# Later places for three steps of the block matching: two transposes and a group of maxima, put one or two turns further on

## The chip, the cores and the metric

The kernel runs on one core of one Trainium2 chip. The metric is the device time of that core in microseconds (us), the median of several executions. One more execution is recorded by the hardware profiler, and all durations below come from that one.

## The reference, cut to what matters

The input `x` holds 8 images of 32 channels with 128 x 128 pixels. The first layer compares every pixel's 3x3 patch with those at the 25 places of a 5x5 window, takes the 8 nearest, gathers their pixels (256 channels), and runs a small convolutional net on them. The second layer is one 5x5 convolution.

```python
def _patch_match_stack(x):
    for dy in range(-2, 3):
        for dx in range(-2, 3):
            sh = x[:, :, yy][:, :, :, xx]                     # shifted, clipped
            d = ((x - sh) ** 2).sum(1, keepdims=True)         # distance
            costs.append(_conv(d, ones, pad=1))               # 3x3 sum
    _, idx = jax.lax.top_k(-jnp.transpose(cost, (0, 2, 3, 1)), 8)
    g = ...                                                   # x at the 8 places
    return ...                                                # [B, 256, H, W]

xb = _patch_match_stack(_gn(x))
dct = _conv(xb, dct_w, groups=32)
h = relu(_conv(_conv(xb, w1), w2, groups=256, pad=1))         # pointwise, depthwise
h = relu(_conv(_conv(h, w3), w4, groups=256, pad=1))
wiener = sigmoid(_conv(_conv(h, w5), w6, groups=256, pad=1))
x = x + _conv(_conv(wiener * dct, inv_dct_w, groups=32), agg_w)
x = x + conv5x5(_gn(x))
```

## The kernel before, in words

**Steps and turns.** The images are worked through one after the other, each in 17 steps of 8 rows. All steps of all images form one list, and the main loop (L1015) goes over it. One step has four **turns** (L1026, `for i in (3, 2, 1, 0)`): turns 3, 2 and 1 do the third, second and first pointwise and depthwise layer, each on a step that lies that much further back, and turn 0 does the last stage. An image thus has 68 turns. In each turn TensorE (PE) has about this order: the pointwise product of the upper 128 channels (`pv`, L641); what the former turn 0 left over (`pa`, L798); then the loose tasks of the queue "P"; in turn 0 the product with the DCT weights (`pc`, L777); the pointwise product of the lower channels (`p`, L665); one unit of the gather (`pg`, L603); and the depthwise layer of the lower channels of the turn before (`pw`, L718). VectorE (DVE) does the depthwise layer of the upper channels: eight multiply-adds on a tile of 128 x 1024 (`acc`, L695), one group in each of the turns 3, 2 and 1. In turn 0 it multiplies `acc` by `pc` (L785). ScalarE (ACT) copies PSUM tiles out, prepares the selection tiles of the gather (L588, L589) and applies the depthwise layer's function (`acc`, L699).

**The order is written out by hand.** PE, DVE and ACT execute their instructions in the order in which the Python program emits them (`manual_schedule(engines=ORDERED)`, L999). Waits between engines follow from the tiles that are written and read. GpSimd (POOL) and SyncE (SP) only issue DMAs and fill borders.

**Loose tasks.** The block matching of the next image is spread over the turns of the current one. It is written as generators. `yield "P", 0` parks a task in the queue for PE, `yield "D", 1.85` in that for DVE with a cost of 1.85 us, `yield "A"` in that for the end of a turn. A third value tells how many turns must go by at least before the task may go on. `run("P")` takes all due tasks of its queue. `tick` (L984) counts a turn, adds an allowance to `owed`, and takes tasks of "D" in their order of arrival until it is spent. In one turn, `run("P")` stands ahead of `tick`. A task that was parked in a tick is taken up by `run("P")` at the start of the next turn.

**The steps around the change.** An image's distances are handled in four chunks (`i` = 0 to 3) of 8 rows in each quarter of the image.

- `costs` loads a chunk's squared differences into `dsum`, waits three turns, and sums 3x3 neighbours on DVE (L477 to L489) by way of a tile `v`. It then transposes the result on PE in two halves of four rows (`pt`, L494, `h` = 0 and 4). ACT copies each half out (`ct`, L498). DVE searches it in four tasks of eight instructions each (`mx` and `idx`, L505 and L506).
- `places` then turns the chunk's indices into addresses on DVE (L520 to L529, tile `oc`), transposes them on PE (`pi`, L538), copies them on ACT (`li`, L540) and stores them with two DMAs from POOL's queue (L541). The gather of the next image reads them back much later.

`v` (L474) and `oc` (L517) are allotted from one pool under one tag with a single buffer:

```python
v = work.tile([P, R, W + 2], F32, name=f"v_{b}_{i}", tag="v", bufs=1)      # L474
oc = work.tile([P, R, W + 2], F32, name=f"oc_{b}_{i}", tag="v", bufs=1)    # L517
```

Only one chunk at a time can be in `dsum`: `held` is set at L459 and cleared when the second half is transposed (L496).

PSUM tiles of PE's products (`pv`, `p`, `pg`, `pa`, `pc`, `pt`, `pi`) come from one pool of five buffers, `ps_x`.

Of the kernel before, what the change touches and what calls it, by code (L numbers as in the profile page):

```python
# [15 lines left out]
P = 128  # L16
# [26 lines left out]
def bm3d_conv_preact(  # L43
# [172 lines left out]
    def push(task):  # L216
        want = next(task, None)
        if want:
            which, cost, *wait = want
            queues[which].append((cost, task, now[0] + (wait[0] if wait else 0)))  # L220
# [181 lines left out]
    def squares(b, i, pd, xn, aa, sq, idx):  # L402
# [48 lines left out]
        if q is not None:  # L451
            push(costs(b, q, sq, idx))

    def costs(b, i, sq, idx):

        yield "A", 0, 2
        while held:
            yield "A", 0, 1
        held.add(b)  # L459

        nc.gpsimd.dma_start(
            dsum[52:100, :, 1 : 1 + W],
            sq[:, :, 8 * i + 2 : 8 * i + 4 + R, 2 : 2 + W].rearrange("o g r x -> (o g) r x"),
        )
        for o in range(13, NO):
            dy, dx = o // 5 - 2, o % 5 - 2
            p = 4 * (NO - 1 - o)
            nc.gpsimd.dma_start(
                dsum[p : p + 4, :, 1 : 1 + W],
                sq[o - 13, :, 8 * i + 2 - dy : 8 * i + 4 + R - dy, 2 - dx : 2 - dx + W],  # L470
            )
        yield "D", 4.6, 3

        v = work.tile([P, R, W + 2], F32, name=f"v_{b}_{i}", tag="v", bufs=1)  # L474
        cost = dsum[:, 0:R, 1 : 1 + W]
        r0 = 1 if i == 0 else 0
        nc.vector.tensor_add(v[:, r0:], dsum[:, r0:R], dsum[:, r0 + 1 : 1 + R])  # L477
        if i == 0:
            nc.vector.scalar_tensor_tensor(
                v[:, 0], dsum[:, 0], inner[:, 0:1], dsum[:, 1], op0=ALU.mult, op1=ALU.add  # L480
            )
        r1 = R - 1 if i == 3 else R
        nc.vector.tensor_add(v[:, :r1], v[:, :r1], dsum[:, 2 : 2 + r1])
        if i == 3:
            nc.vector.scalar_tensor_tensor(
                v[:, r1], dsum[:, R + 1], inner[:, 1:2], v[:, r1], op0=ALU.mult, op1=ALU.add
            )
        nc.vector.tensor_add(cost, v[:, :, 0:W], v[:, :, 1 : 1 + W])
        nc.vector.tensor_add(cost, cost, v[:, :, 2 : 2 + W])  # L489
        for h in range(0, R, 4):  # L490
            yield "P", 0
            pt = ps_x.tile([P, 4, P], F32, name=f"pt_{b}_{i}_{h}", tag="x")
            for q in range(4):
                nc.tensor.transpose(pt[:, q], cost[:, h + q], ident)  # L494
            if h:
                held.clear()  # L496
            ct = work.tile([P, 4, P], F32, name=f"ct_{b}_{i}_{h}", tag="ct")
            nc.scalar.copy(ct[:, :, 0 : 4 * NO], pt[:, :, 0 : 4 * NO])  # L498
            mx = work.tile([P, 16, K], F32, name=f"mx_{b}_{i}_{h}", tag="mx")
            for q in range(4):  # L500
                yield "D", 1.85
                y = 8 * i + h + q
                for rg in range(4):
                    c25 = ct[:, q, rg : rg + 4 * NO - 3 : 4]
                    nc.vector.max(mx[:, 4 * q + rg], c25)  # L505
                    nc.vector.max_index(  # L506
                        idx[:, rg, y // 4, :, y % 4], mx[:, 4 * q + rg], c25
                    )
        push(places(b, idx, i))

    def places(b, idx, i):


        if i == 0:
            idxd[b] = dram.tile([4, 8, K * 4, W], BF16, name=f"idxd_{b}", tag="idxd")
        yield "D", 2.6
        oc = work.tile([P, R, W + 2], F32, name=f"oc_{b}_{i}", tag="v", bufs=1)  # L517
        oc = oc.rearrange("p r w -> p (r w)")
        o, ct = oc[:, 0:256], oc[:, 256:512]
        nc.vector.tensor_copy(  # L520
            o.rearrange("p (g z) -> p g z", g=4),
            idx[:, :, 2 * i : 2 * i + 2].rearrange("p g s k y -> p g (s k y)"),
        )
        nc.vector.tensor_scalar(ct, o, 5.0, None, op0=ALU.is_ge)
        for lim in (10.0, 15.0, 20.0):
            nc.vector.scalar_tensor_tensor(ct, o, lim, ct, op0=ALU.is_ge, op1=ALU.add)
        nc.vector.scalar_tensor_tensor(o, ct, float(QW - 5), o, op0=ALU.mult, op1=ALU.add)
        o3 = o.rearrange("p (s y) -> p s y", y=4)
        nc.vector.tensor_tensor(  # L529
            o3,  # L530
            o3,
            cst[:, C_BASE : C_BASE + 4].unsqueeze(1).to_broadcast([P, 64, 4]),
            ALU.add,
        )
        yield "P", 0
        for h in range(2):
            pt = ps_x.tile([P, 512], F32, name=f"pi_{b}_{i}_{h}", tag="x")
            nc.tensor.transpose(pt[:, :P], o[:, h * P : (h + 1) * P], ident)  # L538
            li = work.tile([P, P], BF16, name=f"li_{b}_{i}_{h}", tag="li")
            nc.scalar.copy(li, pt[:, :P])  # L540
            nc.gpsimd.dma_start(  # L541
                idxd[b][2 * h : 2 * h + 2, 2 * i : 2 * i + 2].rearrange("g s k x -> g (s k) x"),
                li,
            )
        ready.add((b, i))
        if i == 3:
            ready.add(b)
# [451 lines left out]
    with tc.manual_schedule(engines=ORDERED):  # L999
# [15 lines left out]
        for s in range(len(steps) + 2):  # L1015
            if s < len(steps):
                b, n = steps[s]
# [120 lines left out]
```

## Time and profile before

| quantity | value |
|---|---|
| median of 3 runs | 6862.14 us (6855.92 to 6876.67) |
| the profiled execution's own time | 6856.73 us |
| its span, first to last instruction | 6855.0 us |
| granted TensorE clock, mean | 0.974 |
| PE busy | 6362.1 us, 93% of the span |
| DVE busy | 5857.0 us, 85% |
| ACT busy | 5067.7 us, 74% |
| POOL busy | 3250.0 us, 47% |

A share of busy time is a mean over the whole span. What a moved step is worth is read from the place where it stands. Two views serve for that. The waits list pairs of an idle engine and the work that ended its idle time: total us, number of times, longest us. The timeline lists each engine's instructions in order of time: start, length, engine, line, operation, tiles, count, and in brackets the idle time ahead of it and what ended that.

### The profile page before, as it was taken

The page shows a single profiled execution, that of the slowest core. Times are in us where ns is not written, and L with a number is a line of the kernel's source. Part 1 is how long each engine was busy: PE and PEld are TensorE (multiplying, and loading weights), DVE is VectorE, ACT ScalarE, POOL GpSimd, SP SyncE. Part 2 cuts the span into 40 slices and gives each one's busy share as a digit, 9 for nine tenths or more (in the row PEclk, how much of TensorE's full clock was granted, in tenths as well). Part 3 has the DMA queues.
Part 4 walks back from the last instruction along what each step waited for, and adds up shares of the span by engine and source line. Part 5 has one row for each costly group of instructions (what it writes and reads, how often), then busy time and mean ns, then how long its engine had stood idle before and what let it go on. Part 6 is the DMA issues. An engine that isn't in the chain of part 4 may idle for free.

```text
span 6855.0 us, 232443 instructions
## 1 busy us (share of the span) xinstructions
PE 6362.1 (93%) x101090; PEld 2969.2 (43%) x101090; DVE 5857.0 (85%) x8822; ACT 5067.7 (74%) x6698; POOL 3250.0 (47%) x5351
## 2 busy tenths in 40 slices
PE   4698899999999999999999999999999999999997
PEld 1344444444444444444444444444444444444443
DVE  6799988989889898988989888898988889877776
ACT  4687768777687777877778777887768777786772
POOL 6345436544464444644446444464445544344334
PEclk9899999999999999999999999999999999999998
DMA  3566656666566675665656656566665666566553
GB/s 80 134 151 148 155 134 150 163 149 162 149 155 161 147 168 134 167 145 151 165 131 165 160 145 167 134 172 152 151 153 146 161 157 149 137 164 157 148 151 79
DMA packets 809531, 1019.84 MB, mean 149 GB/s; under 512 B 255456, under 2 KB 619936, under 8 KB 808512
## 3 DMA queue, kind: packets, MB, share of 16 engines
q0 software_dynamic: 422432, 745.61, 42.4%
q1 hardware_dynamic: 381056, 256.86, 16.9%
q8 instruction: 796, 13.04, 0.8%
q10 hardware_dynamic: 5024, 2.49, 0.2%
q14 instruction: 223, 1.83, 0.1%
HBM read 553.25 MB, written 217.01 MB: 112 GB/s over the span
## 4 chain that ended last, share of the span: by engine, by line
PE 53%; DVE 20%; DMA 9%; ACT 8%; issue 6%; POOL 3%; SPq 0%; ACTq 0%; POOLq 0%; DVEq 0%
PE pw L718 19%; PE pv L641 13%; DVE acc L695 13%; PE p L665 11%; DMA t<-t 4%; PE pg L603 3%; PE pc L777 2%; PE p L891 2%; DVE idx L506 2%; ACT ib L588 2%; DVE df L413 1%; PE pd L428 1%; ACT df L421 1%; PE pa L798 1%; DVE acc L785 1%
## 5 line engine op out<-in xcount | busy, mean ns | idle before, releaser
L695 DVE SCALAR_TENSOR_TENSOR acc<-tv,dwv,acc 128x1024 f32<-128x1024 f32 (+3 forms) x3264 | 4032.8, 1237 | 255.1 <-ACT acc L692 141.7
L718 PE MATMUL pw<-t,dwd 96*32 96x508 f32 (+6 forms) x19392 | 2161.7, 593 | 137.9 <-DMA t<-t 97.4
L574 POOL DMA_DIRECT2D ib<-idxd x1024 | 571.8, 559 | 1828.0 <-ACT sel L589 1677.2
L718 PEld LDWEIGHTS pw<-t,dwd 96*32 96x32 f32 (+1 forms) x19392 | 715.7, 112 | 1265.5 <-issue 1174.2
L588 ACT ACTIVATE ib<-ib,nplace 128x1024 bf16<-128x1024 bf16 x1024 | 1170.3, 1143 | 19.1 <-DMA ib<-idxd 19.1
L589 ACT ACTIVATE sel<-ib 128x1024 f32<-128x1024 bf16 x1024 | 1084.7, 1059 | 32.5
L665 PE MATMUL p<-acc,lw 128*32 128x256 f32 x16768 | 991.3, 381 | 20.0 <-ACT tv L649 19.5
L641 PE MATMUL pv<-acc,lw 128*128 128x512 f32 (+1 forms) x2112 | 972.0, 602 | 30.2 <-DVE acc L785 22.9
L758 POOL DMA_DIRECT2D xf<-xbd x1088 | 652.8, 634 | 305.3 <-PE pc L777 80.7
L665 PEld LDWEIGHTS p<-acc,lw 128*32 128x32 f32 x16768 | 556.6, 111 | 447.8 <-ACT tv L649 59.5
L649 ACT COPY tv<-pv 128x512 f32<-128x512 f32 (+2 forms) x784 | 439.2, 578 | 403.4 <-PE pv L641 380.6
L603 PEld LDWEIGHTS pg<-sel,xt 128*32 128x32 f32 x45056 | 575.3, 111 | 260.4 <-ACT sel L589 67.1
L421 ACT ACTIVATE df<-df 128x786 f32<-128x786 f32 (+2 forms) x576 | 468.5, 860 | 291.6 <-DVE df L413 288.5
L603 PE MATMUL pg<-sel,xt 128*32 128x48 f32 x45056 | 593.5, 207 | 89.2 <-ACT sel L589 47.6
L731 ACT ACTIVATE acc<-pw 128x512 f32<-128x512 f32 (+2 forms) x808 | 442.7, 573 | 295.7 <-PE pw L718 294.9
L641 PEld LDWEIGHTS pv<-acc,lw 128*128 128x128 f32 x2112 | 380.0, 191 | 524.3 <-issue 404.4
L413 DVE TENSOR_TENSOR df<-xn 128x786 f32<-128x786 f32 (+2 forms) x576 | 527.8, 968 | 82.8 <-PE pd L428 70.9
L699 ACT ACTIVATE acc<-acc 128x1024 f32<-128x1024 f32 (+3 forms) x408 | 416.9, 1022 | 235.4 <-DVE acc L695 235.1
L672 ACT COPY t<-p 128x512 f32<-128x512 f32 x800 | 424.7, 571 | 127.8 <-PE p L665 125.8
L692 ACT ACTIVATE acc<-tv,dwv 128x1024 f32<-128x1024 f32 (+3 forms) x408 | 454.6, 1114 | 57.9 <-PE pa L798 39.1
L641 PE MATMUL pv<-xb,lw 128*128 128x512 f32 x1024 | 474.5, 606 | 0.0
L665 PE MATMUL p<-xb,lw 128*32 128x256 f32 x8192 | 467.6, 380 | 0.0
(151 smaller groups left out, 5778.6 us busy)
## 6 DMA issues: line engine op xcount, KB each, us to landing
ib<-idxd POOLq DMA_DIRECT2D x1024, 256.0 KB, 4.5
xbd<-xb POOLq DMA_DIRECT2D x128, 1024.0 KB, 6.8
xf<-xbd POOLq DMA_DIRECT2D x960, 128.0 KB, 7.0
t<-t SPq DMA_DIRECT2D x792, 128.0 KB
t<-t SPq DMA_DIRECT2D x384, 256.0 KB
tv<-tv SPq DMA_DIRECT2D x384, 130.0 KB
xt<-xtd POOLq DMA_DIRECT2D x240, 176.0 KB, 4.4
xl<-xs POOLq DMA_DIRECT2D x256, 64.0 KB, 2.5
```

Source lines behind the costliest of these rows:

```text
L413: nc.vector.tensor_sub(df[:, :, ca:cz], xn[:, r0 : r0 + SR, ca:cz], xn[:, r0 + dy : r0 + dy + SR, ca + dx : cz + dx],)
L421: nc.scalar.activation(df[:, :, ca:cz], df[:, :, ca:cz], AF.Square)
L574: nc.gpsimd.dma_start(ib.rearrange("p k y x -> p (k y x)"), idxd[b][s4 // 8, s4 % 8, 4 * k0 : 4 * k0 + 8] .rearrange("k x -> (k x)") .part ...
L588: nc.scalar.activation(ib, ib, AF.Square, bias=nplace)
L589: nc.scalar.activation(sel, ib, AF.Relu, scale=-1.0, bias=1.0)
L603: nc.tensor.matmul(pg[C * j : C * (j + 1), :, xa:xz], xt[:, t], sels[j // 2][:, j % 2, :, xa:xz], start=True, stop=True,)
L641: nc.tensor.matmul(ps[:, :hr], lhsT[:, g, P:CK], src(g)[:, h : h + hr], start=g == 0, stop=g == 1,)
L665: nc.tensor.matmul(ps[C * r : C * (r + 1), e, :nb], lhsT[:, g, s], rows[:, r : r + 4 * nb - 3 : 4], start=g == 0, stop=g == 1,)
L692: nc.scalar.activation(acc, rows, AF.Copy, scale=tap)
L695: nc.vector.scalar_tensor_tensor(acc, rows, tap, acc, op0=ALU.mult, op1=ALU.add)
L718: nc.tensor.matmul(pt[u][C * j : C * (j + 1), : nh[u], :nb, xa:xz], dwd[0:hi, i - 1, u, j, dx + 1], t[0:hi, j, : nh[u], :nb, xa + dx : xz ...
L758: nc.gpsimd.dma_start(xf[p : p + C, m, j0:j1], src[g, m, (h + m + 1) % 2, :, :, ya:yz])
```

## The change

Three values are added to three `yield` lines, all for images after the first only (`b` is not 0).

- The transpose of the first half of a chunk's distances (`pt`, `h` = 0) may go on one turn later.
- The first of the four tasks of maxima of each half may go on one turn later. The other three come after it, one by one.
- The transpose of the addresses (`pi`) may go on two turns later, and with it the copies at L540 and the two DMAs at L541.

```diff
         for h in range(0, R, 4):
-            yield "P", 0
+            yield "P", 0, 1 if b and h == 0 else 0
             pt = ps_x.tile([P, 4, P], F32, name=f"pt_{b}_{i}_{h}", tag="x")
...
             for q in range(4):
-                yield "D", 1.85
+                yield "D", 1.85, 1 if b and q == 0 else 0
                 y = 8 * i + h + q
...
-        yield "P", 0
+        yield "P", 0, 2 if b else 0
         for h in range(2):
             pt = ps_x.tile([P, 512], F32, name=f"pi_{b}_{i}_{h}", tag="x")
             nc.tensor.transpose(pt[:, :P], o[:, h * P : (h + 1) * P], ident)
```

No instruction is added or taken away, and no tile changes its size.

## The prediction, made before the changed kernel was run

> **What bounds the kernel now.** I read the page's busy shares and chain first, then the waits list, then the timeline of the places where the moved steps stand.
>
> ```profile
> PE 6362.1 (93%) x101090; PEld 2969.2 (43%) x101090; DVE 5857.0 (85%) x8822; ACT 5067.7 (74%) x6698; POOL 3250.0 (47%) x5351
> ...
> PE 53%; DVE 20%; DMA 9%; ACT 8%; issue 6%; POOL 3%; SPq 0%; ACTq 0%; POOLq 0%; DVEq 0%
> ```
>
> PE carries the time: it is idle for 6855.0 - 6362.1 = 493 us, and nothing that leaves PE's idle time as it is can help. DVE is second, and it leads in a fifth of the chain. The waits list of PE says what that idle time is.
>
> ```profile
> PE pw L718 <- DMA t<-t: 97.4, 39, 5.1
> PE pi L538 <- DVE oc L529: 56.8, 15, 20.2
> ...
> PE pv L641 <- DVE acc L785: 22.9, 15, 2.2
> ```
>
> The second line is what the change is about: PE stands still until DVE has the addresses. But most of it is image 0, which the change leaves alone. The same list from 1400 us on, images 2 to 7, has:
>
> ```profile
> PE pi L538 <- DVE oc L529: 9.0, 8, 1.3
> ```
>
> In between, in image 1, the timeline shows 1.8, 6.7 and 2.8 us. So at most 9.0 + 11.3 = 20 us of waits at `pi` can go. The wait of DVE for `ct` (L505) adds 1.3 us in each later image, and PE has no wait at `pt` there.
>
> Now the place itself: chunk 3 of one image, DVE first. The groups at L695 are one turn's depthwise layer each.
>
> ```profile
> 3303.72 0.43 DVE L529 TENSOR_TENSOR oc<-oc,cst 128x256 f32<-128x256 f32 x1
> 3304.73 1.24 DVE L477 TENSOR_TENSOR v<-dsum 128x1040 f32<-128x1040 f32 x1 [0.59 <-DMA xf<-xbd]
> ...
> 3308.68 1.23 DVE L489 TENSOR_TENSOR dsum<-dsum,v 128x1024 f32<-128x1024 f32 x1
> 3309.82 0.41 DVE L806 TENSOR_TENSOR xr<-xr,pa 128x256 f32<-128x256 f32 x1
> ...
> 3310.61 10.51 DVE L695 SCALAR_TENSOR_TENSOR acc<-tv,dwv,acc 128x1024 f32<-128x1024 f32 x8
> ...
> 3322.76 10.51 DVE L695 SCALAR_TENSOR_TENSOR acc<-tv,dwv,acc 128x1024 f32<-128x1024 f32 x8
> ...
> 3334.86 10.51 DVE L695 SCALAR_TENSOR_TENSOR acc<-tv,dwv,acc 128x1024 f32<-128x1024 f32 x8
> 3345.29 2.47 DVE L785 TENSOR_TENSOR acc<-acc,pc 128x512 f32<-128x512 f32 x4
> ```
>
> DVE has no gap from `v` to L785. PE over the same stretch:
>
> ```profile
> 3304.29 0.41 PE L538 MATMUL pi<-cst,oc 128*128 128x128 f32 x2 [0.51 <-DVE oc L529]
> ...
> 3322.86 3.70 PE L641 MATMUL pv<-xb,lw 128*128 128x512 f32 x8
> 3326.49 3.66 PE L665 MATMUL p<-xb,lw 128*32 128x256 f32 x64
> ...
> 3346.03 3.70 PE L641 MATMUL pv<-acc,lw 128*128 128x512 f32 x8 [1.61 <-DVE acc L785]
> ```
>
> At 3346 PE waits for DVE's first multiplication by `pc`. In this stretch DVE is the slower one, by 1.61 us. The other five later images show 1.6, 0.5, 1.0, 1.2 and 0.1 us there.
>
> **What the Trainium skill says.** "PSUM — Partial Sum Buffer", Engine vs sequencer instructions: "ScalarE/VectorE/GpSimdE queues are strict FIFO". A DVE instruction that waits holds up all behind it. The trace agrees: behind `v`, which started 0.59 us late, nothing overtook. "Perfetto Trace Analysis", Identifying Performance Opportunities: repeating gaps on the engine that should be full can mean too few buffers for the next tile. For PE before, only the tenths to 1.6 us above repeat at this place; what follows is a buffer of this kind that comes free later. "VectorE: DVE Perf Modes", The TRN2 errata: an fp32 add of N elements takes (N+151)/0.96 ns, which for `v` (N = 1040) is 1241 ns; L477 shows 1234. The price of the summing stays.
>
> **The change part by part.** Nothing is added or removed; all is order.
>
> *Transpose of distances, one turn on (28 chunks).* Four products, 0.60 us of PE, stand later, and `ct` (0.47 us on ACT) with them. PE had no wait there, so nothing is gained. `held` still clears with the second half. Cost 0, from -5 to +5 for other neighbours.
>
> *First maxima, one turn on.* Eight instructions of 0.19 + 0.30 us per half move to a turn in which `ct` is surely there. The 1.3 us waits stand ahead of second halves; between these two the same turn count passes as before, so they stay. Gain 0.
>
> *Transpose of addresses, two turns on.* Two products (0.41 us), two copies (0.26 us each), two DMAs of 0.82 us on POOL move past the ib loads (L574) of two turns. The first reader of the new addresses comes three or more turns after the last late store, by the turn numbers of the emission, so no gather waits. What goes is PE's wait at `pi`. What is late next is the buffer: `oc` can't be overwritten until `pi` has read it, and the next `v` has the same buffer.
>
> In the emission of the changed program (turns counted by `tick`) only one pair per image collides. For images 2 to 7, `places` of chunk 2 runs in turn k, `v` of chunk 3 in turn k+1, and `pi` of chunk 2 no longer between them but after tick k+2. So in DVE's order `v` comes first and **waits for PE to come two turns further**. Behind it in DVE's queue stand L806 and three groups L695, 31.5 us of PE's inputs.
>
> The new wait, from the rows above: in PE's order `pi` now follows the `pv` that ended at 3322.86 + 3.70 = 3326.56. Taking away `pi` and its wait (0.92) and `pt` (0.60, now behind `pi`), PE comes there at 3325.0, and `v` starts at about 3325.5, 20.8 us later than at 3304.73. The same reckoning at the other five places (`v` at 1652.5, 2474.9, 4133.5, 4956.9 and 5784.6) gives 21.2, 21.4, 21.2, 20.5 and 22.4. Sum 127.5 us.
>
> How much reaches PE? Two ways lead there, and both do.
> - DVE: `v` to the end of the first L785 is 3346.03 - 3304.73 = 41.3 us without a gap. It ends at 3325.5 + 41.3 = 3366.8, and with it the PSUM buffer that the second half of `pv` takes. The first half finds another and goes ahead, 1.85 us. PE's delay is 20.8 - 1.85 = 19.0 us.
> - ACT: the function at L699 waits for the first group L695, so it starts at `v` + 16.4 us (3321.16 before). Behind it in ACT's queue stand L588, L589, two copies L731 and the copy of `pv` (L649), which ends 4.64 us after L699's start (3325.80 before). In the changed program `p` after `pi` takes the buffer that this copy frees, so PE starts it at 3325.5 + 21.0 = 3346.5. From there to the second half of `pv` are 17.9 + 1.85 us of products: 3366.3. This way gives 18.4, nearly the same, so PE stands in three pieces: 5.2 us at `pt` for `v` to L489, some 15 us at `p`, the rest at `pv`.
>
> L541, behind the late `li`, and L811, behind L806, hold POOL's queue up for about 20 us as well; loads behind them serve units three turns ahead, and PE stands meanwhile. Cost 0, at most +3 per image. SP's shifts (L620, L677) wait for the same layers; same answer.
>
> Six images: 127.5 - 6 x 1.85 = **+116 us**. In these stretches the removed waits at `pi` (9.0 us) give nothing, since DVE, not PE, sets the pace and PE would wait the same time at the next `pv`. Bounds: 6 x 21.5 = 129, and 60 if half the wait is made good by work that I count as late.
>
> *Image 1* is packed closer. There chunk 3 comes ahead of chunk 2, its `v` waits for `pi` of chunk 1: DVE is done with the layer at about 766, PE comes to `pi` at about 775, a wait of 9 us. Against it stand PE's 11.3 us at `pi`, and the chunks' maxima end five turns later, so they press less. I take -5, between -12 and +8. All else in order: 0, ±15.
>
> Sum: +116 - 5 = +111. The profiled execution's own time is 6856.7 (span 6855.0), which gives 6968. The median shown is 5.4 us above that execution, so the forecast for the median is 6862 + 111 = **6973 us**.
>
> **Rivals.**
> 1. *The wait is half hidden.* PE keeps a turn of finished inputs in reserve, so only what goes beyond one turn (827 us an image / 68 = 12.2 us) is lost: 6 x (20.8 - 12.2) = 52, 6914 us. For: a `pv` reads layers of three turns ago. Against: the 1.61 us wait at 3346 says that the reserve is used up there.
> 2. *Faster: the waits at `pi` go and the new wait is hidden.* Then 20 us go, perhaps 8 more of ACT's and POOL's waits behind: 6838 us. It decides if DVE has over 21 us in hand between `v` and L785. For: DVE is idle for 15% of the span. Against: no gap in those 41 us.
> 3. *Nothing to be seen.* The order on the engines doesn't change where it counts, or the two halves cancel: 6862 us. Against: the changed emission differs on all five engines.
> 4. *More.* POOL's queue, held twice, makes a gather late (up to 12 us an image): 6973 + 6 x 5 = 7003.
>
> **How the numbers follow.** A measurement of this kernel can tell about 0.3% (20 us) from no change. My case 0.72, rival 1 0.12, rival 4 0.08: slower 0.92. Rival 2 0.04, rival 3 0.04. The range reaches from rival 1 to just over rival 4: 6912 to 7008.
>
> **What would show it.** In the profile after: a wait of DVE `v` L477 for PE `pi` L538 of some 20 us, six times, about 125 us in all, where 5.8 is listed now; PE waits at `pt` for L489 of 5 us each and at `p` L665 for ACT `tv` L649 of some 15; PE's wait at `pi` from image 1 on near 0; PE busy unchanged near 6360. If that DVE wait is there and the time isn't, step "how much reaches PE" is wrong. If it is missing, the buffer is not shared as I read it.

## The result, and the profile after

| kernel | median, us | runs | ratio to before, 95% interval |
|---|---|---|---|
| before | 6867.76 (6855.92 to 6876.67) | 4 | 1 |
| after | 6971.82 (6951.44 to 6988.81) | 4 | 1.0147 [1.0123, 1.0171] |

The changed kernel is slower by 104 us. Its profiled execution took 6988.81 us (span 6986.9), 17 above its own median. So its spans are set against other profiled executions only with care; what is read below are places inside it.

Against the same line of the page before, PE worked 17 us longer, and its idle time is 6986.9 - 6379.1 = 608 us instead of 493.

```profile
PE 6379.1 (91%) x101090; PEld 2980.0 (43%) x101090; DVE 5855.4 (84%) x8822; ACT 5063.0 (72%) x6698; POOL 3240.9 (46%) x5351
```

The waits list of PE from 1400 us on (images 2 to 7; total us, number, longest). `pi <- oc`, 9.0 us before, has left it. The first line of the list, 18.9 us before, and a new pair, the second line here, each have six waits of one length:

```profile
PE p L665 <- ACT tv L649: 86.6, 6, 14.4
...
PE pt L494 <- DVE xr L806: 33.5, 6, 5.6
PE pv L641 <- DVE acc L785: 25.8, 7, 4.4
```

What ended the idle time ahead of L477 (`v`) on DVE, in the answer for that line:

```profile
  DMA xn<-in_x_dram: 106.0, 5
  PE pi L538: 30.9, 3
...
```

Of these eight waits one, of 0.8 us in image 0, was there before; seven are new. Each is a wait for several semaphores, and the list names the one that came last by the profile. The transfer `xn`, named in five of them, had long been done. In the timeline all seven new waits end at the moment `pi` ends: 9.7 us in image 1, and 20.3, 23.0, 20.4, 22.5, 19.9 and 20.3 us in images 2 to 7, together 126.3 us. Here is the second of those places, first DVE, then PE, then ACT (start, length, engine, line, operation, tiles, in brackets the idle time ahead):

```profile
2499.28 0.43 DVE L529 TENSOR_TENSOR oc<-oc,cst 128x256 f32<-128x256 f32 x1
2522.66 1.24 DVE L477 TENSOR_TENSOR v<-dsum 128x1040 f32<-128x1040 f32 x1 [22.95 <-DMA xn<-in_x_dram]
...
2526.60 1.22 DVE L489 TENSOR_TENSOR dsum<-dsum,v 128x1024 f32<-128x1024 f32 x1
2527.74 0.41 DVE L806 TENSOR_TENSOR xr<-xr,pa 128x256 f32<-128x256 f32 x1
```

```profile
2518.70 3.70 PE L641 MATMUL pv<-xb,lw 128*128 128x512 f32 x8
2522.24 0.38 PE L538 MATMUL pi<-cst,oc 128*128 128x128 f32 x2
2528.21 1.12 PE L494 MATMUL pt<-cst,dsum 128*128 128x128 f32 x4 [5.59 <-DVE xr L806]
2543.77 5.43 PE L665 MATMUL p<-xb,lw 128*32 128x256 f32 x64 [14.44 <-ACT tv L649]
```

```profile
2539.08 1.06 ACT L699 ACTIVATE acc<-acc 128x1024 f32<-128x1024 f32 x1 [24.79 <-DVE acc L695]
...
2543.12 1.08 ACT L649 COPY tv<-pv 128x512 f32<-128x512 f32 x2
```

The addresses are complete at 2499.7. `pi` runs at 2522.24, behind two turns of PE's work. `v` starts when it ends. Then PE stands for want of DVE's and ACT's next results, 5.6 us and, after the transposes, 14.4 us. `pt` waits for L806 and not only for L489, because it takes the PSUM buffer of `pa`, which L806 reads.

### The profile page after: what moved, and what is told of

Same layout as the page of the kernel before. It is cut to its first block, busy times and chain, and to the rows that moved or that the text cites. A ratio compares the mean times of both kernels' runs of the same rounds, so it can differ in the third digit from the quotient of the medians.

```text
span 6986.9 us, 232426 instructions
## 1 busy us (share of the span) xinstructions
PE 6379.1 (91%) x101090; PEld 2980.0 (43%) x101090; DVE 5855.4 (84%) x8822; ACT 5063.0 (72%) x6698; POOL 3240.9 (46%) x5351
## 5 line engine op out<-in xcount | busy, mean ns | idle before, releaser
L665 PE MATMUL p<-acc,lw 128*32 128x256 f32 x16768 | 979.9, 379 | 1.8 <-issue 1.1
L665 PEld LDWEIGHTS p<-acc,lw 128*32 128x32 f32 x16768 | 554.1, 110 | 420.3 <-ACT tv L649 44.1
L421 ACT ACTIVATE df<-df 128x786 f32<-128x786 f32 (+2 forms) x576 | 467.9, 860 | 260.1 <-DVE df L413 257.3
L413 DVE TENSOR_TENSOR df<-xn 128x786 f32<-128x786 f32 (+2 forms) x576 | 527.4, 967 | 84.1 <-PE pd L428 78.2
L665 PE MATMUL p<-xb,lw 128*32 128x256 f32 x8192 | 480.5, 388 | 86.6 <-ACT tv L649 86.6
L672 ACT COPY t<-p 128x512 f32<-128x512 f32 x800 | 423.2, 570 | 126.3 <-PE p L665 124.3
```

Of the source, the lines that this page charges most:

```text
L413: nc.vector.tensor_sub(df[:, :, ca:cz], xn[:, r0 : r0 + SR, ca:cz], xn[:, r0 + dy : r0 + dy + SR, ca + dx : cz + dx],)
L421: nc.scalar.activation(df[:, :, ca:cz], df[:, :, ca:cz], AF.Square)
L665: nc.tensor.matmul(ps[C * r : C * (r + 1), e, :nb], lhsT[:, g, s], rows[:, r : r + 4 * nb - 3 : 4], start=g == 0, stop=g == 1,)
```

## The experiments

**Is it the shared buffer?** Theory A: the delay of `pi` costs through the single buffer under tag "v". Rival: the late addresses cost by themselves.

*e1_own_buffer* gives the addresses a tile of their own; `ct` of `places` stays under "v".

```diff
-        oc = work.tile([P, R, W + 2], F32, name=f"oc_{b}_{i}", tag="v", bufs=1)
-        oc = oc.rearrange("p r w -> p (r w)")
-        o, ct = oc[:, 0:256], oc[:, 256:512]
+        o = work.tile([P, 256], F32, name=f"oc_{b}_{i}", tag="oc", bufs=1)
+        ct = work.tile([P, R, W + 2], F32, name=f"ge_{b}_{i}", tag="v", bufs=1)
+        ct = ct.rearrange("p r w -> p (r w)")[:, 0:256]
```

> The changed kernel, but the addresses `o` have a buffer of their own (128 x 256, tag oc), so that `v` of the next chunk needn't wait for the transpose of the addresses; all three delays stay. Theory (the wait for the shared buffer is the cost): DVE's waits of 20 to 23 us at `v` L477 and PE's at `pt` (5.6 us) and `p` L665 (14.4 us) are gone in images 2 to 7, and the time is about 6850 us (6825 to 6880), back at the kernel before or a little under it. Rival (the late transposes, maxima or addresses cost of themselves, by a longer backlog on DVE or late gathers): it stays at 6950 or more.

6823.13 us, ratio 0.9936 [0.9919, 0.9952]. `pi` is no longer among what L477 waits for; this is the whole list:

```profile
  DMA xl<-xs: 4.9, 1
  DMA dsum<-sq: 2.1, 1
  DMA xf<-xbd: 0.3, 1
```

The slowdown is the buffer's. But the kernel is now faster than before, by a little more than was expected, so something else in the change gains about 40 us.

*e2_chunk2_early* leaves the buffer shared and takes the delay of `pi` from chunk 2 alone, the one whose `pi` falls behind the next `v` in images 2 to 7.

```diff
-        yield "P", 0, 2 if b else 0
+        yield "P", 0, 2 if b and i != 2 else 0
```

> The changed kernel, but the transpose of the addresses of chunk 2 alone goes on without the two turns (chunks 0, 1 and 3 keep them; so do the other two delays). Theory (only the pair `pi` of chunk 2 and `v` of chunk 3 collides in images 2 to 7): the six waits are gone, 6862 us (6835 to 6885); image 1's wait of about 10 us at `v`, which is behind chunk 1, stays. Rival (each chunk's late addresses cost a share): three quarters of the loss stay, about 6945 us.

6849.77 us, ratio 0.9975 [0.9966, 0.9984]. The six waits are gone; one of 10.8 us in image 1 stays, where chunk 3 comes ahead of chunk 2 and chunk 1's `pi` is in its way. So most of the loss is this pair of chunks and not late addresses as such: e2 is 122 us below the changed kernel.

*e3_one_turn* delays `pi` by one turn (`1 if b else 0`).

> The changed kernel with one turn in place of two at the transpose of the addresses. Theory: PE now comes to `pi` after one turn's `p`, `pg` and `pv` (3.7 + 1.1 + 3.7 us), so `v` waits some 8 us in images 2 to 7 and DVE is that late; less the 1.85 us of the half of `pv` that goes ahead, PE loses 6 us an image: 6868 + 37 = 6905 us (6880 to 6930). Rival (any delay past the next `v` costs the whole): 6970. Rival (PE has one turn in reserve): 6868.

6873.39 us, ratio 1.0009 [1.0000, 1.0019], under the expected range, which still counted the other two delays as nothing. The waits of `v` at the six places are now 6.5 to 8.2 us; in the list of L477, most of them:

```profile
  PE pi L538: 38.0, 6
```

A turn less takes 14 us off each wait. At equal other delays (e4 below) the rest, 43.8 us in the six places, costs 6873.4 - 6824.5 = 49 us; 37 were expected.

**Which part gains?** The wait at `pi` was gone in e1, so the first thought was that the gain came from there.

*e4_no_pi_delay* keeps the other two delays and puts `pi` back in its old turn.

> The changed kernel without the delay of the transpose of the addresses; the delays of the distances' transpose and of the maxima stay. Theory (these two cost nothing): 6868 us (6845 to 6890), no wait of 20 us at `v`. Rival (they carry the loss, since they push the chunk's work together on DVE): 6950 or more.

6824.52 us, ratio 0.9938 [0.9920, 0.9955], 43 below the expectation. The gain does not come from `pi`. *e5_pt_only* and *e6_mx_only* keep one delay each:

```diff
-            yield "P", 0
+            yield "P", 0, 1 if b and h == 0 else 0
```

> The kernel before with one of the three delays alone: the transpose of the first half of the distances one turn on. Both delays of distances and maxima together gave 6825 us, 42 below the kernel before. Theory A (the later maxima give that, since DVE does its depthwise group first in the turn and PE gets its inputs sooner): no gain here, 6867 us (6852 to 6880). Theory B (the later transpose gives it, by moving the chunk's whole work on DVE a turn on): 6825. If each gives its half: 6846.

```diff
-                yield "D", 1.85
+                yield "D", 1.85, 1 if b and q == 0 else 0
```

> The kernel before with the delay of the first maxima of each half alone. Theory A (the later maxima give the gain): 6825 us (6812 to 6842). Theory B (the later transpose of the distances does): 6867. Half each: 6846.

e5: 6824.49 us, ratio 0.9949 [0.9933, 0.9965]. e6: 6865.33 us, ratio 1.0003 [0.9994, 1.0012]. The delay of the transpose of distances alone brings the gain; that of the maxima does nothing.

*e7_pi_alone_own* is the kernel before with the delay of `pi` alone, and the buffer of e1.

> The kernel before with the delay of the addresses' transpose by two turns alone, and with a buffer of its own for `o`, so that the next `v` needn't wait. Theory (late addresses are harmless, and the waits of PE at `pi` in images 1 to 7, 20 us, go only where DVE is not the slower one): 6855 us (6840 to 6870). Rival (the delay of the addresses costs of itself, in POOL's queue or in the gathers): 6885 or more. Rival (it gives the full gain of the run with a buffer of its own): 6825.

6871.84 us, ratio 1.0013 [1.0005, 1.0021], 2 us above the expected range. Freed of the buffer the delay of `pi` still gains nothing. More waits for SP's shifts appear in PE's list than before (97.4 us in 39 there, and 104.1 in 43 in the control e9 below):

```profile
PE pw L718 <- DMA t<-t: 138.5, 63, 6.1
```

*e9_own_buffer_before* is the control: the buffer of e1 and no delay.

> The kernel before with the addresses' tile in a buffer of its own, no step moved. If the shared buffer costs only where `pi` is late (theory A), nothing waits for it here, except the wait of 0.6 us ahead of some `v`: no change, 6865 us, between 6855 and 6870. If the buffer of its own had itself brought the gain of e1_own_buffer (rival), the time would be near 6825 us.

6868.9 us, ratio 1.0009 [0.9999, 1.0018]. The buffer itself brings nothing. e7 differs from this control by the delay of `pi` alone, and by 0.0004 in the ratio: the delay without the collision has no effect that these runs can tell from zero.

**Where does the delay of `pt` gain?** *e10_pt_image_1* has it in image 1 alone (`b == 1 and h == 0`), *e11_pt_later_images* in images 2 to 7 (`b > 1 and h == 0`).

> The kernel before with the transpose of distances one turn on in image 1 alone. If the 40 us of e5_pt_only come from image 1 (theory 1: there the chunks are packed closest), 6825 us. If they come from the copy `tv` L649 that in images 2 to 7 stood behind `ct` in ACT's queue at the place of chunk 3 (theory 2), only image 1's own change of some 11 us in the profile is left: 6854 us.

> The same in images 2 to 7 alone. Theory 1: 6865 us, no change. Theory 2: the six waits of PE at `p` L665 for ACT's `tv` L649 (18.9 us before) go and some new waits at `pg` come: 6836 us, that is, 29 of the 40 us. If the two parts do not add up to 40, one changes what the other finds.

e10: 6851.55 us, ratio 0.9985 [0.9976, 0.9994]. e11: 6843.81 us, ratio 0.9969 [0.9960, 0.9979]. Both parts gain, 10 and 21 us by the ratios, together 31 of e5's 35. Theory 2 is nearer, with less than its 29 us in the later images.

**Does the slowed clock matter?** In the long pause of PE the granted clock falls, and `p` (L665) after it takes 5.0 to 6.6 us at the six places instead of 3.7. Before e8 this looked like the missing term: some 13 us. *e8_pe_kept_warm* fills the pause with extra products into the tile of the transpose, ahead of the transposes that then overwrite it.

```diff
+            for _ in range(22 if b > 1 and i == 3 and h == 0 else 0):
+                nc.tensor.matmul(
+                    pt.rearrange("p q x -> p (q x)"), ident,
+                    band[:, 0:4].rearrange("p a x -> p (a x)"),
+                    start=True, stop=True,
+                )
             for q in range(4):
                 nc.tensor.transpose(pt[:, q], cost[:, h + q], ident)
```

> The changed kernel with 22 matrix products more in images 2 to 7, between `pi` of chunk 2 and `pt` of chunk 3, into the PSUM tile that `pt` overwrites next: some 13 us of work for PE in the stretch where it stands and waits for ACT's copy anyway. Theory (PE's idle stretch of 14.4 us lowers the granted clock, and the products after it take 5.0 to 6.6 us for the 3.7 that they take at full clock): `p` after the wait is back at 3.7 us, the mean granted clock near 0.97, and the time 13 us lower, 6959 us, though PE has more to do. Rival (the clock is no cost, the products wait for operands): 6972 or more, `p` stays above 5 us.

6998.48 us, ratio 1.0210 [1.0188, 1.0232]: a miss. The timeline of PE shows why (lines stand 8 further on in this kernel; L494 are the extra products, each of which the trace has as two):

```profile
2515.22 21.23 PE L494 MATMUL pt<-band,cst 128*128 128x512 f32 x44 [5.59 <-DVE xr L814]
2536.29 0.60 PE L502 MATMUL pt<-cst,dsum 128*128 128x128 f32 x4
2536.82 3.66 PE L673 MATMUL p<-xb,lw 128*32 128x256 f32 x64
```

`v` started at 2509.7, so ACT's copy was there at about 2530.8 (21.1 us later, as in the changed kernel). The extra products overran it by 6 us, 36 us over the six places, so this run doesn't decide. *e12_warm_shorter* has 13 of them.

> The changed kernel as in e8_pe_kept_warm, with 13 instead of 22 extra products into the tile of the transpose ahead of `pt` of chunk 3 in images 2 to 7. In e8 22 took 21.2 us, so 13 should take some 12.5 us and end about 1 us before ACT's copy is done. If the slow clock after the idle stretch is the missing 13 us (theory A), `p` L665 takes 3.7 us instead of 5.0 to 6.6 and the time is 6959 us, 12 below the changed kernel. If the extra products only add work or the clock's part is made good later (rival), 6972 us or more.

6980.90 us, ratio 1.0177 [1.0153, 1.0201]. This interval overlaps that of the changed kernel; the 12 us less do not appear. The products fit this time, and `p` is quick:

```profile
2512.76 13.56 PE L494 MATMUL pt<-band,cst 128*128 128x512 f32 x26 [5.59 <-DVE xr L814]
2526.15 0.60 PE L502 MATMUL pt<-cst,dsum 128*128 128x128 f32 x4
2528.31 3.66 PE L673 MATMUL p<-xb,lw 128*32 128x256 f32 x64 [1.56 <-ACT tv L657]
...
2596.94 6.40 PE L649 MATMUL pv<-acc,lw 128*128 128x512 f32 x8 [4.41 <-DVE acc L793]
```

The last line says where it went. `v` began at 2507.2; 89.7 us later PE waits 4.4 us for DVE's product with `pc` of the next step. The changed kernel has the same wait 89.8 us after its `v` (2522.7), although its `p` was slower:

```profile
2612.42 5.30 PE L641 MATMUL pv<-acc,lw 128*128 128x512 f32 x8 [4.36 <-DVE acc L785]
```

And in e4, where nothing was delayed at `v` (2456.7), it stands at +90.0 us:

```profile
2546.69 5.40 PE L641 MATMUL pv<-acc,lw 128*128 128x512 f32 x8 [2.09 <-DVE acc L785]
```

From `v` to this point DVE sets the pace in all three: its only wait of over 0.3 us there is one of 1.0 to 2.1 us, ahead of maxima (L505). What PE loses or gains in between is levelled out there. Over the six places PE goes on at +90.2 us on average in the changed kernel and at +89.7 in e12. An estimate from these figures: the slow clock costs about 6 x 0.5 = 3 us, not 13. The medians are too noisy to show so little.

## Why the prediction was right, and where not

Forecast 6973 us, 111 more than before; measured 6971.82, 104 more than before. The new wait, its place and its length came as forecast. That the total is so near is luck: the gain of one step was missed by some 35 to 43 us, and what the delay of `pi` costs was put too low by nearly as much.

**The bound and the new wait.** As predicted, DVE's `v` waits for PE's `pi` once in each of images 2 to 7; 126.3 us against about 125. PE's first two pieces came as worked out: 5.6 us at `pt` (5.2), 14.4 at `p` (15), and `p` starts 21.1 us after `v` (21.0). The third piece, a rest at the next `pv`, did not come at once: PE, slowed by its clock, reached it after DVE (in e12, at full clock, PE does wait there, 0.1 to 0.3 us). It came a step later, at about +90 us.

**How much reaches PE: the credit of 1.85 us was wrong.** The prediction gave PE back 1.85 us per image, for the first half of `pv` that goes ahead. The wait at +90 us takes such a lead away again. From one `v` (chunk 2) to the next (chunk 3) the six intervals are 114.7 to 117.9 us in the changed kernel and 95.5 to 96.7 in e4, 122.1 us longer in all; which is about the 126.3 less the 0.6 us of waiting that each had already. The medians of the changed kernel and e2 differ by as much. The other intervals from `v` to `v` in the later images agree within 1 us on average, so nothing is made good. Predicted for these six: `v` later by 127.5, of which 116 reach PE. The lateness was 5 us smaller, and all of it reaches PE.

**Image 1: the number about held, the reason did not.** Predicted: -5 us net, between -12 and +8, of a wait of 9 us at `v` against the waits at `pi` that go. The wait came (9.7 us). The changed kernel, e8 and e12 have the same instructions up to the first `v` of image 2. It starts at 1204.5, 1200.0 and 1198.2 us in their profiles. In the kernel before and e11, where image 1 is as it was, it starts at 1201.8 and 1196.8. So the net is small. But what pays for the wait is not what the prediction named. In e4 and e5, without the delay of `pi`, this `v` starts at 1186.5 and 1187.6: the delay of `pi` costs 11 to 18 us up to here. The waits at `pi` give little back: `v` starts at 1194.6 in e7, without them, and at 1197.6 in e9, with them. What pays is the transpose of distances: 1188.9 in e10, which has its delay in image 1 alone, and 10 us less by that run's ratio.

**The transpose of distances: "Cost 0, from -5 to +5" failed.** Alone it gains 35 us [24, 46] by the ratio of e5. The prediction looked at PE's wait at `pt`, found none and went no further. The second half of a chunk comes after the first, so `held` clears a turn later too, and the next chunks fall into other turns. In the profiles, `v` follows `v` within a later image after 157, 169 and 124 us before, and after 193, 157 and 96 in e5. That moves a thing on another engine: ACT squares the differences of the chunks further on (L421), in queue order, and waits there for DVE's L413. ACT's waits from 1400 to 6700 us, before and in e5:

```profile
ACT df L421 <- DVE df L413: 208.7, 57, 10.5
```

```profile
ACT df L421 <- DVE df L413: 174.6, 46, 7.2
```

Before, one such wait of 6.0 to 10.5 us stood in each later image some 52 us ahead of the `v` of chunk 3, and behind it in ACT's queue the copy that PE's `p` needs. PE's list, whole run, before and in e5:

```profile
PE p L665 <- ACT tv L649: 19.5, 7, 3.7
```

```profile
PE p L665 <- ACT tv L649: 0.6, 1, 0.6
```

That these waits go is shown. That they are the 21 us of e11 is not: PE's wait `pg <- acc L785` (25.4 us in 6) comes in their place in e5, and PE's idle time ahead of its instructions from 1100 us on is 260 us before and 262 in e5. In e7 the wait at `p` goes as well (2.4 us in 2 are left), and nothing is gained. In image 1 the profile does show the gain: PE's idle time from its first instruction up to 1100 us falls from 187 to 171. The rest of the difference between the two profiles is in PE's busy time, 6362.1 us before, 6350.4 in e5 and 6352.6 in e11, for the same products; but it is 6364.0 in e4, which has the same delay of `pt`. Where the later images' share comes from stays open.

**The steps put at nothing.** The maxima: 0, and e6 shows 0. The waits at `pi` that go: nothing gained, and e7 and the equality of e1 and e4 (6823 and 6825) show it. POOL's queue, "0, at most +3 per image": e1 has the late stores on POOL and is as quick as e4, so 0. In e7 the same stores come with 9 us more [3, 14] and more waits at `pw`, but the control e9 has 6 us more [-1, 12] without them, so no cost of the stores is shown.

**The sum.** By the ratios the changed kernel loses 101 us [84, 117] and e4 gains 43 [31, 55], so the delay of `pi` costs 144, give or take 20, where 111 were forecast. The runs divide it: the medians give 122 us to chunk 2's delay (e2) and 25 to the rest, where 116 and -5 were forecast. In the 25 are image 1's wait (the first `v` of image 2 starts at 1194.8 in e2, 8 us after e4) and the late addresses of the other chunks, or noise. The profiled spans of the changed kernel and e4 differ by 148.3: 122.1 at the six waits, 21.1 ahead of chunk 2's `v` in image 2, 5.1 elsewhere. e8 and e12, with the same instructions up to that `v`, are only 10.4 and 8.5 us behind e4 there, so about half of the 21.1 belongs to that one execution.

**The rivals.** "Half hidden" falls: each `v` is 20 us late and so is everything after it. "Faster" was right that something gains 40 us, though not at `pi`, and wrong that the new wait is hidden. "More", by POOL, has e1 against it.

A version that beats both kernels needs only the first of the three delays: e5, 6824.49 us. With all three and the buffer of its own it is 6823.13 (e1), the same within the intervals.

## What to carry to other kernels

When a reader is moved further on, look first at who writes its buffer next: with a single buffer the next writer, and all that is queued behind it, moves with the reader. Follow a delay to the next place at which the pacing engine is waited for in both kernels: here the leads and lags of PE ended there, and only DVE's delay went on. And of a step in a chain of turns, ask what clears after it: a moved release moves everything that waits for it, on engines that the diff doesn't name.

## What the runs showed of the hardware that was not expected

PE's clock follows its pauses. The windows of the changed kernel (stretch, its us, busy us of PE, PEld, DVE, ACT and POOL, clock, DMA share, GB/s), the pause and the stretches after it:

```profile
2529.40:2543.80 14.40, 0.03 (x4) 0.04 (x6) 14.04 (x12) 4.69 (x7) 3.58 (x8) 0.50 0.10 27
2543.80:2549.20 5.40, 5.40 (x82) 2.76 (x86) 5.26 (x5) 4.84 (x8) 2.27 (x3) 0.67 0.46 87
2549.20:2555.00 5.80, 5.80 (x136) 2.55 (x124) 5.49 (x27) 4.71 (x6) 0.56 (x1) 1.00 0.51 117
```

In e12 the clock is back ahead of `p`:

```profile
2526.70:2532.00 5.30, 3.74 (x85) 2.33 (x88) 5.16 (x5) 5.23 (x11) 2.17 (x3) 1.00 0.24 76
```

The Trainium skill, "TensorE: Matmul & The Clock Gate", What's actually happening, says that an idle window of about 3.4 us throttles the array to half its clock, and that about as much sustained work releases it, with a spread from run to run. The trace agrees: 0.50 in the pause, and `p` took 5.0 to 6.6 us instead of 3.66, that is 1.3 to 3.0 us more, so it ran 2.7 to 5.9 us at half speed (an estimate, twice the extra time). It differs in the length of the pause. In e4 the `pv` after a wait of only 2.09 us, shown above, took 5.40 us, and the granted clock over its stretch was 0.68:

```profile
2546.69:2552.10 5.41, 5.41 (x12) 2.11 (x16) 1.74 (x3) 3.99 (x6) 1.27 (x3) 0.68 1.10 220
```

So here about 2 us of waiting were enough. What the prediction would have gained by knowing this is small: about 3 us in all, since DVE's pace covered the rest.
